# Causal attention in a four-batch transformer kernel: mask inside the row maximum, quotients formed in the transposed layout

## The chip, the cores and the metric

The kernel runs on one core of a Trainium2 chip. The metric is the device time of one execution in microseconds (us); lower is better. One core has TensorE (PE, matrix products, its results go to PSUM banks of 128 partitions by 512 f32 values), VectorE (DVE), ScalarE (ACT), GpSimd (POOL), SyncE (SP) that issues transfers, and DMA engines. Each engine runs its own queue of instructions in order and waits for others through semaphores.

## The reference

Four sequences of 1024 tokens with 256 channels go through two transformer layers in f32, each followed by a residual sum and layer norm.

```python
x = _layernorm(x + _L0_attn_ref(x, ...))   # 16 heads of 16, no mask, q and k normed, rope
x = _layernorm(x + _L0_ffn_ref(x, ...))    # SiLU gate, 256 -> 768 -> 256
x = _layernorm(x + _L1_attn_ref(x, ...))   # 8 heads of 32, causal
x = _layernorm(x + _L1_ffn_ref(x, ...))    # 16 experts, two per token, at most 512 tokens each
```

The change concerns the third line mostly:

```python
def _L1_attn_ref(x, w_qkv, w_out, head_scales):
    B, T, C = x.shape                      # 4, 1024, 256
    H = N_HEADS                            # 8
    hd = C // H                            # 32
    scale = 1.0 / math.sqrt(hd)
    qkv = (x @ w_qkv).reshape(B, T, 3, H, hd)
    q = jnp.transpose(qkv[:, :, 0], (0, 2, 1, 3))
    k = jnp.transpose(qkv[:, :, 1], (0, 2, 1, 3))
    v = jnp.transpose(qkv[:, :, 2], (0, 2, 1, 3))
    scores = jnp.einsum('bhqd,bhkd->bhqk', q, k) * scale
    causal = jnp.tril(jnp.ones((T, T), dtype=bool))
    scores = jnp.where(causal[None, None], scores, -jnp.inf)
    q_proj = jnp.einsum('bhtd,hd->bht', q[..., :3], dirs)
    k_proj = jnp.einsum('bhtd,hd->bht', k[..., :3], dirs)
    geo = q_proj[..., :, None] * k_proj[..., None, :]
    scores = scores + head_scales[None, :, None, None] * geo
    attn = jax.nn.softmax(scores, axis=-1)
    out = jnp.einsum('bhqk,bhkd->bqhd', attn, v).reshape(B, T, C)
    return out @ w_out
```

The geometric term is a product of one number per query and one per key, so the kernel folds it into the query projection's weights, and the products of q and k already hold it.

## The kernel before, in words

All instructions up to the experts are ordered by hand: the order in which the program is written is the order in each engine's queue. A stage is a generator of "units" (some PE work with what hangs on it), and `weave` (L1145) runs the units of one stage and puts the "pieces" of another between them: each call of a piece issues a few matrix products and their followers. `later(n, fn)` (L116) puts a small step of DVE or POOL on a list; `tick` (L119), once per unit, issues the steps that are due. PSUM has eight banks: a ring of six, tag "s", that nearly all products take in turn, and one each for values and denominators (`ps_av`, `ps_m`).

The four batches pass one after the other through first attention (`first_units`, L1051), second attention (`second_units`, L1103), the SiLU FFN and the routing; `weave` joins one batch's attention with the other pieces of its own batch or of a neighbour. Near the end, L1344 weaves batch 3's second attention, with projection and routing pieces of batch 2 in it and, from unit 30, the first pieces of batch 3's own projection and routing. L1348 issues what is left before the last tokens are sent to the experts.

A second attention works on two groups of four heads. It has 36 units:

- Twelve head units (a "head" below is this opening stretch of an attention, not an attention head): `Maxima1.unit` of group 0 alone.
- Twelve units of group 0: the scores (L969), values (L1004) and, beside them, the maxima of group 1.
- Twelve units of group 1: scores and values alone.

`Maxima1.unit` (L923) forms, for 128 queries and up to 512 keys of four heads, the products in four banks (L931). Units on the diagonal (8 of 12, with 128, 256, 384 or 512 keys) then add a triangle of large negative numbers to the last 128 columns, by one matrix product of `ident_h` and `mask_h` per head (L940). DVE takes the negated row maximum of each bank into `part` (L942). `split` and `turn` put the maxima into a layout in which PE subtracts them as part of the scores.

`scores` lays keys on partitions and 512 queries along the bank; ACT takes the exponential (L989) into `pe`, POOL clears what lies above the diagonal (L992). `values` (L1015) adds up two banks over the key blocks: the value products `av`, with heads and channels on partitions and tokens along the bank, and the denominators `dn` in the same layout, each repeated over the 32 channels of its head. After the last key block ACT copies both banks to SBUF (L1025). `unload` (L1028), one or two units later, turns them with eight PE transposes into a layout with tokens on partitions (L1033), DVE takes the reciprocal of the denominators (L1036) and multiplies (L1037) into `oq1`.

`out_project` (L540) serves both layers. A "turn" transposes four blocks of the quotients back to channels on partitions (L549) and ACT copies them (L552); a "project" multiplies by the output weights (L559), and `add_residual` (L515) adds on DVE and starts the layer norm.

At the start of the program `project_qk` squares q and k on POOL (L230) and sums the squares on DVE (L233); the square has one buffer, tag "sq", which the sine table also uses.

Of the kernel before, what the change touches and what calls it, by code (L numbers as in the profile page):

```python
# [35 lines left out]
def postln_layers_kernel(ctx: ExitStack, tc: tile.TileContext, a: dict, out: bass.AP):  # L36
# [8 lines left out]
    mask_h = const.tile([P, P], BF16, name="mask_h")  # L45
    nc.gpsimd.memset(mask_h, 0.0)
    nc.gpsimd.affine_select(
        out=mask_h, in_=mask_h, pattern=[[-1, P]], compare_op=ALU.is_ge, fill=NEG, base=0, channel_multiplier=1
    )
    neg_half = const.tile([P, 1], F32, name="neg_half")  # L50
# [51 lines left out]
    with ExitStack() as main:  # L102
# [45 lines left out]
        sinT = fa.tile([P, TB, D0], F32, tag="sq", bufs=1, name="sinT")  # L148
# [54 lines left out]
        def project_qk(b, pr, first=False):  # L203


            def piece(j, big):
# [21 lines left out]
                def squares():  # L228
                    sq = fa.tile([P, 512], F32, tag="sq", bufs=1, name=f"sq0_{b}_{pr}_{j}")
                    nc.gpsimd.tensor_tensor(sq, x, x, ALU.mult)  # L230

                    def sums():
                        nc.vector.tensor_reduce(part, sq.rearrange("p (h d) -> p h d", d=D0), AX.X, ALU.add)  # L233

                    return sums
# [135 lines left out]
        class Maxima:  # L371


            def __init__(self, b, g, engines):
# [7 lines left out]
                def rotate(s, u):  # L382
# [3 lines left out]
                    y = fa.tile(  # L386
                        [P, 4, 4, D0], F32, tag="tmp" if eng is nc.gpsimd else "sq", bufs=1, name=f"y0_{b}_{g}_{s}_{u}"
                    )
# [123 lines left out]

        mvs, open_rows = {}, set()
# [26 lines left out]
        def out_project(b, oqs, w, name):  # L540
# [3 lines left out]
            def turn(h, c, big):  # L544
                if c == 0:
                    oTs[h] = act.tile([P, 2, 512], F32, tag="hT", bufs=1, name=f"oT{name}_{b}_{h}")
                pt = bank(f"pt{name}_{b}_{h}_{c}", big)
                for i in range(4):
                    nc.tensor.transpose(  # L549
                        pt[:, i * P : (i + 1) * P], oqs[b][:, 4 * h + i, c * P : (c + 1) * P], ident  # L550
# [3 lines left out]
            def project(j, big):  # L554
                ps = bank(f"pp{name}_{b}_{j}", big)
                for i in range(2):
                    q = slice((2 * j + i) % 4 * P, ((2 * j + i) % 4 + 1) * P)
                    for c in range(2):
                        nc.tensor.matmul(  # L559
                            ps[:, i * 256 : (i + 1) * 256], oTs[j // 2][:, c, q], w[:, c, :], start=c == 0, stop=c == 1  # L560
                        )
                for i in range(2):
                    add_residual(b, 2 * j + i, ps[:, i * 256 : (i + 1) * 256], name)
# [5 lines left out]
            return out  # L569

# [302 lines left out]
        def wait(big):  # L873
            pass

# [39 lines left out]
        class Maxima1:  # L915
# [7 lines left out]
            def unit(self, i):  # L923
# [5 lines left out]
                for h in range(4):  # L929
# [6 lines left out]
                        stop=not diag,  # L936
                    )
                if diag:
                    for h in range(4):
                        nc.tensor.matmul(scs[h][:, n - P : n], ident_h, mask_h, start=False, stop=True)  # L940
                for h in range(4):
                    nc.vector.tensor_reduce(self.part[:, t, u, h : h + 1], scs[h][:, :n], AX.X, ALU.max, negate=True)  # L942
# [20 lines left out]
        class Attend1:  # L963


            def __init__(self, m, oq):
                self.m, self.oq, self.b, self.g, self.pes, self.avs = m, oq, m.b, m.g, {}, {}
# [36 lines left out]
            def values(self, i):  # L1004
# [17 lines left out]
                if kt == 4 * qb + 3:  # L1022
                    for k in range(2):
                        d = act.tile([P, 512], F32, tag="avs", bufs=2, name=f"avs1_{self.b}_{self.g}_{qb}_{k}")
                        nc.scalar.copy(d, self.av[k])  # L1025
                        self.avs[qb, k] = d

            def unload(self, qb):  # L1028
                pt = [ps_s.tile([P, 512], F32, tag="s", name=f"pto1_{self.b}_{self.g}_{qb}_{k}") for k in range(2)]
                for k in range(2):  # L1030
                    for t in range(4):
                        q = slice(t * P, (t + 1) * P)
# [515 lines left out]
```

## Time and profile before

| | us |
|---|---|
| runs | 2515.32, 2517.42, 2521.31 |
| median | 2517.42 |
| the profiled execution | 2514.16 |
| its span in the profile | 2512.3 |
| around the span (difference) | 1.9 |
| PE busy in the span | 2360.3 (94%) |
| DVE busy | 1366.7 (54%) |
| ACT busy | 1023.4 (41%) |
| POOL busy | 730.5 (29%) |

The profile is of one execution. Its mean granted clock of PE is 0.959 of full speed. A group line of the profile reads: code line, engine, operation, output<-input with partitions x elements, number of instructions, then busy time and mean ns of one, then the idle time of the engine just before them and who ended it. In the time line, the first number is the start and the second the duration of one instruction or of a run of equal ones (the last field gives how many), and the brackets hold the idle time before it. A wait line gives who waited for whom, total us, how often, and the longest.

### The profile page before, as it was taken

Reading aid. Unit: us, or ns where it says so; the run is one execution under the profiler, and the core shown is the slowest. Engines: PE = TensorE matmul, PEld = TensorE weight load, DVE = VectorE, ACT = ScalarE, POOL = GpSimd, SP = SyncE. Lnnn points to the kernel's source line nnn. Section 1 sums busy time; section 2 is a strip of 40 time slices with the busy share of each in tenths; the row PEclk is TensorE's granted clock in tenths of the full one; section 3 lists DMA queues with packets and bytes.
Section 4 is the critical chain, followed back from the end, with each engine's and each line's share of the span. In section 5 each row is a group of like instructions: output and inputs, shape, how many; then the busy total and the mean of one; then the engine's idle time right before and its main releaser. Section 6 shows DMA issues by size and latency. Waiting matters only on the chain.

```text
span 2512.3 us, 36681 instructions
## 1 busy us (share of the span) xinstructions
PE 2360.3 (94%) x14452; PEld 1193.2 (47%) x14452; DVE 1366.7 (54%) x3161; ACT 1023.4 (41%) x2011; POOL 730.5 (29%) x1015
## 2 busy tenths in 40 slices
PE   6999999999999999999999999999999983999994
PEld 3333334444445543444455434445556442666662
DVE  6765654766657447787563677817535565111113
ACT  1355554555552345545424455472331340111112
POOL 5623623425024112454131320211110143112223
PEclk8999999999998999999989999999998985999997
DMA  3134212000000000001100000102000012444434
GB/s 89 33 120 136 82 61 83 1 27 1 1 1 27 1 1 1 23 24 54 31 1 1 1 1 1 41 28 98 1 1 1 1 52 68 101 101 118 103 88 145
DMA packets 79628, 109.89 MB, mean 44 GB/s; under 512 B 8800, under 2 KB 68448, under 8 KB 77792
## 3 DMA queue, kind: packets, MB, share of 16 engines
q1 hardware_dynamic: 54080, 80.21, 9.8%
q0 software_dynamic: 9984, 14.82, 3.1%
q10 hardware_dynamic: 15392, 12.53, 1.7%
q8 instruction: 113, 1.85, 0.3%
q14 instruction: 59, 0.48, 0.1%
HBM read 68.64 MB, written 38.90 MB: 43 GB/s over the span
## 4 chain that ended last, share of the span: by engine, by line
PE 85%; DVE 8%; POOL 2%; DMA 2%; issue 1%; ACT 1%; SPq 0%; ACTq 0%; POOLq 0%; DVEq 0%
PE sc L458 19%; PE av L476 10%; PE ph L1410 7%; PE py L1426 7%; PE gu L595 7%; PE mx L434 4%; PE sc L978 4%; PE mx L931 4%; PE p L898 4%; PE dn L611 4%; PE av L1015 3%; PE dn L1015 2%; DVE part L942 2%; PE qk L298 2%; PE ppa L559 2%; PE pt L425 2%
## 5 line engine op out<-in xcount | busy, mean ns | idle before, releaser
L437 DVE TENSOR_REDUCE part<-mx 128x1 f32<-128x512 f32 x1024 | 656.3, 684 | 340.6 <-PE mx L434 334.8
L467 ACT ACTIVATE pe<-sc 128x512 f32<-128x512 f32 x1024 | 554.1, 596 | 392.9 <-PE mx L434 338.0
L434 PE MATMUL mx<-kT,qT 32*128 32x512 f32 x2048 | 650.3, 643 | 5.7 <-DVE part L437 5.5
L458 PE MATMUL sc<-qT,kT 32*128 32x512 f32 x2048 | 614.6, 636 | 0.2 <-ACT pe L467 0.2
L458 PEld LDWEIGHTS sc<-qT,kT 32*128 32x128 f32 x2048 | 181.7, 183 | 223.1 <-issue 177.0
L476 PE MATMUL av<-pe,va 128*32 128x512 f32 x2048 | 272.7, 605 | 0.0
L942 DVE TENSOR_REDUCE part<-mx 128x1 f32<-128x512 f32 (+3 forms) x384 | 186.8, 549 | 152.2 <-PE mx L940 108.6
L434 PEld LDWEIGHTS mx<-kT,qT 32*128 32x128 f32 x2048 | 196.5, 184 | 53.6 <-DVE part L437 28.2
L989 ACT ACTIVATE pe<-sc 128x512 f32<-128x512 f32 (+3 forms) x384 | 157.6, 499 | 156.6 <-PE sc L978 156.4
L1410 PE MATMUL ph<-dmT,f 128*128 128x512 f32 x384 | 170.2, 602 | 4.3 <-DVE dmT L90 3.5
L1426 PE MATMUL py<-f,hTm 128*128 128x256 f32 x768 | 167.7, 379 | 0.0
L1418 ACT ACTIVATE hTm<-ph,b 128x512 f32<-128x512 f32 x96 | 60.8, 684 | 261.3 <-PE ph L1410 261.3
L992 POOL TENSOR_SCALAR_AFFINE_SELECT pe<-pe 128x256 f32<-128x256 f32 x128 | 51.9, 412 | 373.9 <-ACT pe L989 371.7
L1426 PEld LDWEIGHTS py<-f,hTm 128*128 128x128 f32 x768 | 145.9, 190 | 25.0 <-issue 5.7
L1430 POOL DMA_INDIRECT acc_d<-yo,dm x48 | 74.5, 1553 | 284.8 <-DVE yo L1428 238.9
L931 PE MATMUL mx<-kT,qT 32*128 32x512 f32 (+3 forms) x768 | 138.6, 592 | 8.2 <-DVE part L942 4.8
L356 POOL TENSOR_TENSOR ss<-ss,neg_half 128x16 f32<-128x16 f32 x48 | 138.8, 2909 | 0.5
L1427 DVE TENSOR_TENSOR yo<-py,b 128x256 f32<-128x256 f32 x48 | 20.4, 425 | 210.3 <-PE py L1426 210.3
L476 PEld LDWEIGHTS av<-pe,va 128*32 128x32 f32 x2048 | 40.3, 108 | 192.6 <-issue 182.6
L978 PE MATMUL sc<-qT,kT 32*128 32x512 f32 (+3 forms) x768 | 118.3, 547 | 1.7 <-DVE part L942 0.6
L1410 PEld LDWEIGHTS ph<-dmT,f 128*128 128x128 f32 x384 | 72.8, 192 | 94.8 <-issue 86.7
L595 PE MATMUL gu<-xTf,wg 128*128 128x256 f32 x384 | 106.8, 400 | 0.0
(357 smaller groups left out, 2935.2 us busy)
## 6 DMA issues: line engine op xcount, KB each, us to landing
f<-in_fc SPq DMA_DIRECT2D x14, 1024.0 KB, 5.0
f<-in_fc ACTq DMA_DIRECT2D x10, 1024.0 KB, 5.7
xink<-in_xT SPq DMA_DIRECT2D x32, 256.0 KB, 3.7
disp_d<-empty SPq DMA_DIRECT2D x12, 520.0 KB, 6.1
qk_d<-xs SPq DMA_DIRECT2D x6, 1024.0 KB, 4.3
xr<-qk_d SPq DMA_DIRECT2D x6, 1024.0 KB
dm<-disp_d SPq DMA_DIRECT2D x11, 520.0 KB, 3.6
xinv<-in_xT SPq DMA_DIRECT2D x16, 256.0 KB, 4.8
```

The costliest lines, as they stand in the source:

```text
L434: nc.tensor.matmul(sc, self.qT[r, t * P : (t + 1) * P], self.kT[r, u * 512 : (u + 1) * 512], start=True, stop=True)
L437: return lambda: nc.vector.tensor_reduce(self.part[:, t, u, h : h + 1], sc, AX.X, ALU.max, negate=True)
L458: nc.tensor.matmul(sc, self.m.kT[r, kt * P : (kt + 1) * P], self.m.qT[r, qb * 512 : (qb + 1) * 512], start=True, stop=True)
L467: nc.scalar.activation(self.pes[i, h // 2][:, h % 2, :], sc, AF.Exp)
L476: nc.tensor.matmul(self.av[32 * h : 32 * h + 32, :], va0[:, kt, 4 * self.g + h, :], self.pes[i, h // 2][:, h % 2, :], start=kt == 0, stop= ...
L595: nc.tensor.matmul(ps[:, i * 256 : (i + 1) * 256], w[:, c, f * P : (f + 1) * P], xT[j][:, c, :], start=c == 0, stop=c == 1,)
L931: nc.tensor.matmul(scs[h][:, :n], qT[r, t * P : (t + 1) * P], kT[r, u * 512 : u * 512 + n], start=True, stop=not diag,)
L942: nc.vector.tensor_reduce(self.part[:, t, u, h : h + 1], scs[h][:, :n], AX.X, ALU.max, negate=True)
L978: nc.tensor.matmul(scs[h][:, off:], ones_h[r, :] if w else kT[r, kt * P : (kt + 1) * P], (self.m.nmT if w else qT)[r, q], start=w == 0, st ...
L989: nc.scalar.activation(pe[:, j, off:], scs[2 * hp + j][:, off:], AF.Exp)
L1410: nc.tensor.matmul(ph[:, i * CAP : (i + 1) * CAP], f1[:, c, (f + i) * P : (f + i + 1) * P], dmT[:, c, :], start=c == 0, stop=c == 1,)
L1426: nc.tensor.matmul(py[:, :C], hT[:, f, c * P : (c + 1) * P], f2[:, f, :], start=f == 0, stop=f == FF1 // P - 1)
```

## The change

- The mask joins the row maximum. A constant `mask_w` of 128x512 holds zeros and, in its last 128 columns, the triangle. On diagonal units DVE adds it to the bank and takes the maximum in one call, `tensor_tensor_reduce` (add, scale by -1, minimum), whose elementwise result goes to a scratch tile `masked` that nobody reads. In the instruction stream a call is two DVE instructions, the main one and one that reads the accumulator out. The 256 mask products on PE are gone.
- The quotients are formed where the value products lie. `unload` is gone. ACT copies denominators, then values, to SBUF, and in the following units four `divide` steps, a quarter (128 tokens) each, take a reciprocal of 128x128 on DVE and multiply on POOL, into `oT1`, with channels on partitions.
- The second layer's projection reads `oT1` directly. Its turns and their ACT copies are gone; two empty pieces take their place in the order. `out_project` becomes `out_project0` (first layer, unchanged in what it issues) and `out_project1`.
- The squares, the sine table and one rope product move from a tag with one buffer to a tag with two.

```diff
     make_identity(nc, ident)
-    mask_h = const.tile([P, P], BF16, name="mask_h")
-    nc.gpsimd.memset(mask_h, 0.0)
+
+    mask_w = const.tile([P, 512], BF16, name="mask_w")
+    nc.gpsimd.memset(mask_w, 0.0)
     nc.gpsimd.affine_select(
-        out=mask_h, in_=mask_h, pattern=[[-1, P]], compare_op=ALU.is_ge, fill=NEG, base=0, channel_multiplier=1
+        out=mask_w[:, 384:512],
+        in_=mask_w[:, 384:512],
+        pattern=[[-1, P]],
+        compare_op=ALU.is_ge,
+        fill=NEG,
+        base=0,
+        channel_multiplier=1,
     )
+    masked = const.tile([P, 512], BF16, name="masked")
     neg_half = const.tile([P, 1], F32, name="neg_half")
...
         nc.scalar.dma_start(cosT, a["cos"].rearrange("(t p) d -> p t d", p=P))
-        sinT = fa.tile([P, TB, D0], F32, tag="sq", bufs=1, name="sinT")
+        sinT = act.tile([P, TB, D0], F32, tag="q1", bufs=G1, name="sinT")
         nc.scalar.dma_start(sinT, a["sin"].rearrange("(t p) d -> p t d", p=P))
...
                 def squares():
-                    sq = fa.tile([P, 512], F32, tag="sq", bufs=1, name=f"sq0_{b}_{pr}_{j}")
+                    sq = act.tile([P, 512], F32, tag="q1", bufs=G1, name=f"sq0_{b}_{pr}_{j}")
                     nc.gpsimd.tensor_tensor(sq, x, x, ALU.mult)
...
                     x = xr[:, ts, s, hs, :]
-                    y = fa.tile(
-                        [P, 4, 4, D0], F32, tag="tmp" if eng is nc.gpsimd else "sq", bufs=1, name=f"y0_{b}_{g}_{s}_{u}"
-                    )
+                    if eng is nc.gpsimd:
+                        y = fa.tile([P, 4, 4, D0], F32, tag="tmp", bufs=1, name=f"y0_{b}_{g}_{s}_{u}")
+                    else:
+                        y = act.tile([P, 4, 4, D0], F32, tag="q1", bufs=G1, name=f"y0_{b}_{g}_{s}_{u}")
                     z = fa.tile([P, 4, 4, D0], F32, tag="tmpz", bufs=1, name=f"z0_{b}_{g}_{s}_{u}")
...
+        def wait(big):
+            pass
+
...
-        def out_project(b, oqs, w, name):
+        def project_out(b, j, oT, w, name, big):
+
+            ps = bank(f"pp{name}_{b}_{j}", big)
+            for i in range(2):
+                for c in range(2):
+                    nc.tensor.matmul(
+                        ps[:, i * 256 : (i + 1) * 256], oT(c, i), w[:, c, :], start=c == 0, stop=c == 1
+                    )
+            for i in range(2):
+                add_residual(b, 2 * j + i, ps[:, i * 256 : (i + 1) * 256], name)
+
...
+        def out_project1(b):
+
+
+            def project(j, big):
+                project_out(b, j, lambda c, i: oT1[b][:, c, (2 * j + i) * P : (2 * j + i + 1) * P], w1o, "a1", big)
+
+            out = [lambda big, j=j: project(j, big) for j in range(4)]
+            return out[:2] + [wait, wait] + out[2:]
...
                         start=True,
-                        stop=not diag,
+                        stop=True,
                     )
-                if diag:
-                    for h in range(4):
-                        nc.tensor.matmul(scs[h][:, n - P : n], ident_h, mask_h, start=False, stop=True)
                 for h in range(4):
-                    nc.vector.tensor_reduce(self.part[:, t, u, h : h + 1], scs[h][:, :n], AX.X, ALU.max, negate=True)
+                    part = self.part[:, t, u, h : h + 1]
+                    if diag:
+                        nc.vector.tensor_tensor_reduce(
+                            masked[:, :n], scs[h][:, :n], mask_w[:, 512 - n :], -1.0, -NEG, ALU.add, ALU.min, part
+                        )
+                    else:
+                        nc.vector.tensor_reduce(part, scs[h][:, :n], AX.X, ALU.max, negate=True)
...
-            def __init__(self, m, oq):
-                self.m, self.oq, self.b, self.g, self.pes, self.avs = m, oq, m.b, m.g, {}, {}
+            def __init__(self, m, oT):
+                self.m, self.oT, self.b, self.g, self.pes = m, oT, m.b, m.g, {}
...
                 if kt == 4 * qb + 3:
-                    for k in range(2):
-                        d = act.tile([P, 512], F32, tag="avs", bufs=2, name=f"avs1_{self.b}_{self.g}_{qb}_{k}")
-                        nc.scalar.copy(d, self.av[k])
-                        self.avs[qb, k] = d
-
-            def unload(self, qb):
-                pt = [ps_s.tile([P, 512], F32, tag="s", name=f"pto1_{self.b}_{self.g}_{qb}_{k}") for k in range(2)]
-                for k in range(2):
-                    for t in range(4):
-                        q = slice(t * P, (t + 1) * P)
-                        nc.tensor.transpose(pt[k][:, q], self.avs[qb, k][:, q], ident)
-                p4 = [t.rearrange("p (t h d) -> p t h d", t=4, h=4) for t in pt]
-                rc = act.tile([P, 4, 4], F32, tag="rc", bufs=2, name=f"rc1_{self.b}_{self.g}_{qb}")
-                nc.vector.reciprocal(rc, p4[1][:, :, :, 0])
-                nc.vector.tensor_tensor(
-                    self.oq[:, 4 * qb : 4 * qb + 4, P * self.g : P * self.g + P].rearrange(
-                        "p t (h d) -> p t h d", h=4
-                    ),
-                    p4[0],
-                    rc.unsqueeze(3).to_broadcast([P, 4, 4, D1]),
-                    ALU.mult,
-                )
+
+                    vs, rc = [
+                        act.tile([P, 512], F32, tag="avs", bufs=2, name=f"{n}_{self.b}_{self.g}_{qb}")
+                        for n in ("avs1", "rc1")
+                    ]
+                    nc.scalar.copy(rc, self.av[1])
+                    nc.scalar.copy(vs, self.av[0])
+
+                    def divide(k):
+                        q = slice(k * P, (k + 1) * P)
+                        nc.vector.reciprocal(rc[:, q], rc[:, q])
+                        to = self.oT[:, self.g, qb * 512 + k * P : qb * 512 + (k + 1) * P]
+                        nc.gpsimd.tensor_tensor(to, vs[:, q], rc[:, q], ALU.mult)
+
+                    for k in range(4):
+                        later(min(1 + k, 3), lambda k=k: divide(k))
         groups = {}
-        oq0, oq1, ends = {}, {}, {}
+        oq0, oT1, ends = {}, {}, {}
         both_pool = (nc.gpsimd, nc.gpsimd)
...
-            oq1[b] = act.tile([P, TB, C], F32, tag="oq", bufs=2, name=f"oq1_{b}")
+            oT1[b] = act.tile([P, G1, S], F32, tag="oq", bufs=2, name=f"oT1_{b}")
             now = Maxima1(b, 0)
...
                 nxt = Maxima1(b, g + 1) if g + 1 < G1 else None
-                at = Attend1(now, oq1[b])
+                at = Attend1(now, oT1[b])
                 for i in range(12):
...
                         now.turn(1)
-                        if last is not None:
-                            last.unload(1)
                     if nxt is not None:
...
                             nxt.split(1)
-                    if i == 6:
-                        at.unload(0)
                     yield
             last.values(11)
-            last.unload(1)
...
         def first_end(b):
-            return [lambda big: ends[b](big)] + out_project(b, oq0, w0p, "a0")
+            return [lambda big: ends[b](big)] + out_project0(b)
         def second_end(b):
-            return out_project(b, oq1, w1o, "a1") + route(b)
+            return out_project1(b) + route(b)
...
         out2 = second_end(2)
-        straight(out2[:8] + project1(3))
-        out3 = out_project(3, oq1, w1o, "a1")
+        straight(out2[:6] + project1(3))
+        out3 = out_project1(3)
         st, tu, lo = route(3, True)
         steps2, sums2 = dispatch(2, True)
-        weave(second_units(3), 23, out2[8:], True, out3[:4] + st[:2], 30, steps2, 18)
+        weave(second_units(3), 23, out2[6:], True, out3[:2] + [wait] + st[:2], 31, steps2, 18)
         flush()
-        for piece in tu[:2] + out3[4:6] + lo[:2] + out3[6:]:
+        for piece in tu[:2] + lo[:2] + out3[4:]:
             piece(True)
```

More of the change, by code (lines that the diff above doesn't have):

```diff
@@ L538, in add_residual, with out_project0 @@
                 later(1, root)
-        def out_project(b, oqs, w, name):
+        def project_out(b, j, oT, w, name, big):
[7 more added lines that the diff above has]
+                add_residual(b, 2 * j + i, ps[:, i * 256 : (i + 1) * 256], name)
+        def out_project0(b):
             oTs = {}
@@ L545, in turn @@
                 if c == 0:
-                    oTs[h] = act.tile([P, 2, 512], F32, tag="hT", bufs=1, name=f"oT{name}_{b}_{h}")
-                pt = bank(f"pt{name}_{b}_{h}_{c}", big)
+                    oTs[h] = act.tile([P, 2, 512], F32, tag="hT", bufs=1, name=f"oTa0_{b}_{h}")
+                pt = bank(f"pta0_{b}_{h}_{c}", big)
                 for i in range(4):
                     nc.tensor.transpose(
-                        pt[:, i * P : (i + 1) * P], oqs[b][:, 4 * h + i, c * P : (c + 1) * P], ident
+                        pt[:, i * P : (i + 1) * P], oq0[b][:, 4 * h + i, c * P : (c + 1) * P], ident
                     )
@@ L554, in project, with oT @@
             def project(j, big):
[L555 to L560, printed above, removed]
-                        )
-                for i in range(2):
-                    add_residual(b, 2 * j + i, ps[:, i * 256 : (i + 1) * 256], name)
+                def oT(c, i):
+                    t = (2 * j + i) % 4
+                    return oTs[j // 2][:, c, t * P : (t + 1) * P]
+                project_out(b, j, oT, w0p, "a0", big)
             out = []
@@ L871, in postln_layers_kernel @@
         sent, based = [], []
-        def wait(big):
-            pass
         qTs, kTs, va1 = {}, {}, {}
@@ L1022, in values @@
                 if kt == 4 * qb + 3:
-                    for k in range(2):
-                        d = act.tile([P, 512], F32, tag="avs", bufs=2, name=f"avs1_{self.b}_{self.g}_{qb}_{k}")
-                        nc.scalar.copy(d, self.av[k])
-                        self.avs[qb, k] = d
-            def unload(self, qb):
-                pt = [ps_s.tile([P, 512], F32, tag="s", name=f"pto1_{self.b}_{self.g}_{qb}_{k}") for k in range(2)]
-                for k in range(2):
-                    for t in range(4):
-                        q = slice(t * P, (t + 1) * P)
-                        nc.tensor.transpose(pt[k][:, q], self.avs[qb, k][:, q], ident)
-                p4 = [t.rearrange("p (t h d) -> p t h d", t=4, h=4) for t in pt]
-                rc = act.tile([P, 4, 4], F32, tag="rc", bufs=2, name=f"rc1_{self.b}_{self.g}_{qb}")
-                nc.vector.reciprocal(rc, p4[1][:, :, :, 0])
-                nc.vector.tensor_tensor(
-                    self.oq[:, 4 * qb : 4 * qb + 4, P * self.g : P * self.g + P].rearrange(
-                        "p t (h d) -> p t h d", h=4
-                    ),
-                    p4[0],
-                    rc.unsqueeze(3).to_broadcast([P, 4, 4, D1]),
-                    ALU.mult,
-                )
+                    vs, rc = [
[11 more added lines that the diff above has]
+                        later(min(1 + k, 3), lambda k=k: divide(k))
         groups = {}
-        oq0, oq1, ends = {}, {}, {}
+        oq0, oT1, ends = {}, {}, {}
         both_pool = (nc.gpsimd, nc.gpsimd)
```

## The prediction

> **What bounds the kernel now.** I read the page first (shares of busy time, the chain that ended last, the costliest groups), then busy time by stretch around the second attention, then the waits of VectorE and TensorE there, then single instructions.
>
> ```profile
> span 2512.3 us, 36681 instructions
> PE 2360.3 (94%) x14452; PEld 1193.2 (47%) x14452; DVE 1366.7 (54%) x3161; ACT 1023.4 (41%) x2011; POOL 730.5 (29%) x1015
> PE 85%; DVE 8%; POOL 2%; DMA 2%; issue 1%; ACT 1%; SPq 0%; ACTq 0%; POOLq 0%; DVEq 0%
> ```
>
> TensorE (PE) is busy 94% of the span and holds 85% of the chain, so work taken off its queue normally shortens the run by that work. VectorE (DVE) holds the next 8%; the change loads that engine, so the stages where it is near its limit decide. Busy time by stretch: the "heads" of batches 0 to 3 (the twelve units of maxima that open a second attention), then of batch 0 its first and second head group:
>
> ```profile
> 756.80:789.00 32.20, 30.87 (x169) 17.89 (x165) 25.72 (x63) 4.03 (x7) 15.62 (x8) 0.84 0.16 51
> 1238.60:1272.80 34.20, 32.87 (x168) 18.98 (x164) 25.73 (x63) 4.03 (x7) 15.64 (x8) 0.75 0.18 56
> 1696.80:1735.20 38.40, 35.88 (x217) 22.86 (x214) 34.64 (x91) 4.67 (x9) 3.74 (x8) 0.96 0.45 159
> 1914.50:1948.90 34.40, 32.51 (x161) 19.86 (x160) 29.27 (x78) 1.76 (x3) 2.80 (x6) 0.75 0.00 0
> 789.00:862.00 73.00, 72.17 (x588) 35.18 (x592) 42.36 (x107) 28.83 (x68) 18.86 (x28) 0.98 0.01 1
> 862.00:915.00 53.00, 52.44 (x436) 29.24 (x428) 12.18 (x31) 21.83 (x54) 7.38 (x18) 1.00 0.00 1
> ```
>
> The columns are the window, its length, and the busy time of PE, weight loads, DVE, ACT and POOL, then PE's granted clock. In the heads DVE is busy 75 to 90% and the clock is 0.75 to 0.96: PE and DVE hand six banks to and fro. In the group stretches PE is full (72 of 73 us, 52 of 53) and DVE has room (42, then 12). One instruction more on DVE is near its full price in a head and near nothing behind it.
>
> **The change part by part.** (a) Masks. 256 mask matmuls, four per diagonal unit, leave PE. What a unit's four cost is read from the starts in the time line:
>
> ```profile
> 833.62 0.40 PE L940 MATMUL mx<-mask_h,ident_h 128*128 128x128 bf16 x4
> 833.86 0.65 PE L595 MATMUL gu<-xTf,wg 128*128 128x256 f32 x2
> 827.07 1.09 PE L1033 MATMUL pto<-ident,avs 128*128 128x128 f32 x8
> 828.00 1.03 PE L595 MATMUL gu<-xTf,wg 128*128 128x256 f32 x4
> 921.31 0.66 PE L549 MATMUL pta<-ident,oq 128*128 128x128 f32 x4
> 921.90 0.69 PE L458 MATMUL sc<-qT,kT 32*128 32x512 f32 x1
> ```
>
> Start to next start: 0.24 us a mask group, 0.93 us a turn of the quotients (L1033), 0.59 us a turn ahead of the projection (L549). Of 64 diagonal units 32 lie in group stretches where PE is full: 32 x 0.24 = 7.7 us gained.
>
> In the same units the row maximum becomes tensor_tensor_reduce, built as two DVE instructions: the add with the mask, and a read of the accumulator; the former also waits for the previous write of its scratch tile. The plain reduce:
>
> ```profile
> L942 DVE TENSOR_REDUCE part<-mx 128x1 f32<-128x512 f32 x192 | 119.1, 682 | 53.8 <-PE mx L931 43.3 <-PE mx L940 10.4
> L942 DVE TENSOR_REDUCE part<-mx 128x1 f32<-128x256 f32 x64 | 22.6, 417 | 13.8 <-PE mx L940 13.7
> ```
>
> The trace has no tensor_tensor_reduce. Call D the extra time of one masked maximum. Four 512-wide reduces take 2.48 us (start 763.62), 0.60 apart, so consecutive ones overlap by 0.08. A two-input operation on a bank and SBUF costs what a one-input one does (L520, 256 wide, 407 ns; the 256-wide reduce 417 ns). Lower end: only the read is added, as the copy of 128x4 between two row operations at 2025.38, for 0.07 us of queue; with 0.04 to 0.05 for lost overlap D = 0.12. Upper end: no overlap, both steps whole with a gap of 0.04 each: 0.68 + 0.04 + 0.17 + 0.04 - 0.60 = 0.33; I use 0.31, since the narrow forms have less to lose. I take D = 0.17, by the copy's row, which is nearest to a read of one value.
>
> Here a rule speaks against the change. The Trainium skill, page "VectorE: DVE Perf Modes", section "The DRAIN you can't avoid", says that a DVE operation does not start until the pipe of the one before has emptied, and its "Rules for kernel authors" ask for few operations rather than few waits. By that D is its upper end, 0.31. The trace's overlap of 0.08 and slot of 0.07 for a 0.16 us copy say that small followers cost less, so the row decides for the centre and the rule supplies the first rival. With 0.31 the sum below would be a loss.
>
> Heads: 4 x 32 x 0.17 = 21.8 us more DVE. Back come DVE's waits for masks:
>
> ```profile
> DVE part L942 <- PE mx L940: 4.3, 6, 2.2
> DVE part L942 <- PE mx L940: 5.1, 6, 2.2
> DVE part L942 <- PE mx L940: 19.9, 3, 18.4
> DVE part L942 <- PE mx L940: 23.2, 3, 22.3
> ```
>
> One line per head, batches 0 to 3; the longest is the wait before the head's first unit and stays, so 2.1 + 2.9 + 1.5 + 0.9 = 7.4 us. The mask groups also stand on PE ahead of later units; at the heads' clock one is 0.3 us, 32 are 9.6, and I count half, 4.8, because DVE also waits for the plain products there (3.2 us in the first head). Net loss 21.8 - 7.4 - 4.8 = 9.6 us.
>
> (b) Quotients. The 16 turns of eight go. Fifteen stand in full PE stretches: 15 x 0.93 = 14.0 us, and PE's wait for the copies ahead of them (pto on avs, 2.2 us by the waits) mostly goes: 1.7. The sixteenth is in the tail, under (e). In their place ScalarE copies the same two banks, in the other order: the value bank comes free some 0.6 us later. Its next user comes after the next unit's scores on PE, over 4 us, so nothing; without that cover 16 x 0.6 = 10 us. Per turn 0.255 + 0.692 = 0.95 us of DVE goes (L1036, L1037), and four reciprocals of 128x128 come. The exact shape has a row, 953 ns (L249), so 64 x 0.953 - 16 x 0.95 = 61.0 - 15.2 = +45.8 us of DVE. Each of 64 new POOL multiplies is as L393, 464 ns: 30 us on an engine at 29%. Affine selects queue behind them and values behind those; POOL has 50 us free of 73, so I give it nothing (16 x 0.5 = 8 us if one per turn were exposed). The quarters are due within three ticks and the two buffers are wanted again four or five units later, so ScalarE's next copies don't wait.
>
> (c) Exposed DVE work outside the heads: 45.8 + 128 x 0.17 = 67.6 us, beside full PE. PE's own waits on DVE are small there (none among those of batch 0's two groups), and DVE keeps 30 us free per group stretch. But a reciprocal of 1 us sits ahead of maxima whose banks PE wants. Ends: nothing, and half (34 us). I take a tenth, 6.8, nearer the lower end as the six banks give about one unit of slack.
>
> (d) Projection. Of 16 second-layer turns (L549) 14 leave full stretches: 14 x 0.59 = 8.3 us; their ScalarE copies (588 ns each) lay beside. Projections now depend on POOL's products, one stage behind their quarter; the two empty pieces keep the distance. Nothing, or 0.5 us each at 16 projections, 8 us, if POOL were late.
>
> (e) Ends. At the start, squares lie in one buffer:
>
> ```profile
> 12.99 1.04 POOL L230 TENSOR_TENSOR sq<-xr 128x512 f32<-128x512 f32 x1 [8.49 <-DVE rope_x L177]
> 18.51 1.04 POOL L230 TENSOR_TENSOR sq<-xr 128x512 f32<-128x512 f32 x1 [4.48 <-DVE ss L233]
> 20.42 1.04 POOL L230 TENSOR_TENSOR sq<-xr 128x512 f32<-128x512 f32 x1 [0.86 <-DVE ss L233]
> 22.32 1.04 POOL L230 TENSOR_TENSOR sq<-xr 128x512 f32<-128x512 f32 x1 [0.86 <-DVE ss L233]
> ```
>
> With two, POOL need not wait 0.86 us per square, and the sine table no longer shares: the last sum should end about 21.2 instead of 24.1, 2.9 us on a serial chain. The DMA that loads the table keeps its place in ScalarE's queue; the wider mask costs POOL a longer fill while it waits 8.49 us anyway. At the end of batch 3 one turn of quotients and two ahead of the projection go from the chain that leads to routing: 0.93 + 2 x 0.59 = 2.1; I count 2.0, as POOL's sends stand before its last products.
>
> **Sum.** Gains 7.7 + 14.0 + 1.7 + 8.3 + 2.9 + 2.0 = 36.6; losses 9.6 + 6.8 = 16.4; net 20.2. The profiled execution took 2514.16, of which 1.9 lie around the span of 2512.3; it becomes 2494.0 with a span of 2492.1. It stands 3.3 under the median of 2517.42, from which the same step gives 2497.
>
> **Rivals.** *VectorE becomes the bound.* Place: the heads. Price: at D = 0.31 they lose 39.7 - 12.2 = 27.5; outside, 39.7 us of masked maxima, half exposed as PE starves for banks, 19.9; reciprocals 6.8 as nothing better is known; less 36.6, so +17.6, 2535. It decides from about D = 0.25 (19.8 + 12.8 + 6.8 = 39.4 against 36.6, at four tenths exposed). For it: DVE at 90% in the third head, the added wait on the scratch tile, the rule above. Against: 0.07 us for a small copy. Chance 0.22, spread 2518 to 2540.
>
> *Freed PE time turns into waits.* PE stops less for masks and turns, but sooner for banks, exponentials and selects; half the gain stays: 36.6/2 = 18.3, less the heads' 9.6, so -8.7: 2509. For it: affine selects already hold values up (4.4 us by the waits). Against: ACT is at 40% and POOL at 26% of the group stretch. Chance 0.12.
>
> *The change doesn't remove what it says:* excluded for PE, since the changed code issues no mask product and no second-layer turn; only the start's 2.9 and the tail's 2.0 could fail (2502).
>
> **How the numbers follow.** Forecast 0.66, own range 2484 to 2511: below, D = 0.12 and nothing exposed, 6 + 7 us; above, D = 0.22 or 14 us exposed. About 0.2% (5 us) is what a measurement of this kernel can tell from no change. Of the forecast 0.63 is faster and 0.03 within; of the second rival 0.09 faster, 0.02 within, 0.01 slower; of the first 0.02 within, 0.20 slower. The range 2482 to 2526 leaves out 0.05 below and some 0.13 of the first rival above.
>
> **What would show it.** Accumulator reads near 0.17 us or less and four masked 512 maxima in 3.0 to 3.3 us: right; above 3.6, first rival. Heads 2 to 3 us longer each. Batch 0's first group stretch about 4 us shorter with PE still 97% busy; a fall to 93% with waits of mx on part or of av on pe would be the second rival. Reciprocals at 0.95 us; last start-up sum at 21 us. Wrong altogether if the masked maximum runs at half rate (1.2 us for 512): at a mean width of 320 and (682 - 417)/256 = 1.04 ns an element 128 x 0.33 = 43 us more in the heads alone.

## The result, and the profile after

The changed kernel takes 2537.22 us (median of 4 runs, 2536.97 to 2539.80) against 2517.56 us before (4 runs): 1.0084 times as long, 95% interval 1.0072 to 1.0096. The prediction was 2497 us and faster; the time lies outside its range.

The head of the page after, and the chain by engine:

```profile
span 2535.3 us, 36343 instructions
PE 2367.6 (93%) x14004; PEld 1181.4 (47%) x14004; DVE 1430.7 (56%) x3449; ACT 1015.3 (40%) x1995; POOL 761.8 (30%) x1079
PE 83%; DVE 10%; POOL 2%; DMA 2%; issue 1%; ACT 1%; ACTq 0%; SPq 0%; DVEq 0%; POOLq 0%
```

Two of these numbers seem to contradict each other: PE has 448 matmul records fewer and is busy 7 us longer. So a matmul's busy time in this profile is not work alone. The 384 products of 512 columns for the maxima (L931 before, L956 after) are the same in both kernels and show 726 ns each before, 797 after.

The medians differ by 19.7 us, the spans of the two profiled executions by 23.0. The table says where the 23 us went, worked out from the starts of the stages in both traces. A head here ends at the first exponential of its attention, and the second group begins with its own first exponential. "Between" is from the end of the last product of values and denominators of one second attention to the first product for the maxima of the next; for the most part this is the next batch's first attention.

| stage | before | after, difference |
|---|---|---|
| start and first attention of batch 0 | 756.8 | -4.2 |
| the four heads | 153.3 | +12.2 |
| first groups, four | 270.2 | +3.5 |
| second groups, batches 0 to 2 | 170.8 | -4.1 |
| second group, batch 3 | 43.1 | +3.2 |
| the three stretches between | 662.5 | +12.3 |
| from there to the end | 455.5 | +0.1 |

The heads of batches 0 to 3 by the windows' busy time (PE, weight loads, DVE, ACT, POOL, then PE's granted clock), and below them batch 3's head before. PE shows as busy for 92 to 97% of each, its clock is down to 0.55 in batch 3's head (0.73 before), and DVE has some 8 us free at most:

```profile
752.70:792.10 39.40, 38.13 (x152) 22.85 (x148) 31.86 (x105) 4.62 (x8) 16.80 (x10) 0.68 0.13 42
1242.80:1282.30 39.50, 38.21 (x152) 22.68 (x148) 31.36 (x102) 4.65 (x9) 16.81 (x10) 0.70 0.15 49
1707.60:1754.70 47.10, 43.11 (x214) 26.38 (x210) 41.19 (x134) 5.32 (x11) 3.74 (x8) 0.96 0.37 130
1929.80:1969.20 39.40, 38.16 (x141) 22.24 (x140) 33.05 (x113) 1.76 (x3) 2.80 (x6) 0.55 0.00 1
```

```profile
1914.50:1952.10 37.60, 35.71 (x177) 21.59 (x176) 31.85 (x86) 2.35 (x4) 2.80 (x6) 0.73 0.00 1
```

The new instructions' groups, and below them DVE's time line in the first head, after and then before:

```profile
L966 DVE CUSTOM_DVE_ANT_0 masked<-mx,mask_w 128x512 bf16<-128x512 f32 x64 | 44.2, 691 | 16.3 <-PE mx L956 8.8
L966 DVE DVE_READ_ACCUMULATOR2_ANT part<- 128x1 f32 x256 | 21.3, 83 | 0.1
L1061 DVE RECIPROCAL rc<-rc 128x128 f32<-128x128 f32 x64 | 58.1, 929 | 12.8 <-ACT rc L1056 7.8 <-POOL pe L1020 5.1
L1063 POOL TENSOR_TENSOR oT<-avs,rc 128x128 f32<-128x128 f32 x64 | 29.5, 462 | 154.1 <-DVE rc L1061 148.0 <-DVE lg L719 4.5 <-DVE lg L808 1.1
```

```profile
760.52 0.69 DVE L966 CUSTOM_DVE_ANT_0 masked<-mx,mask_w 128x512 bf16<-128x512 f32 x1
761.14 0.08 DVE L966 DVE_READ_ACCUMULATOR2_ANT part<- 128x1 f32 x1
761.36 0.69 DVE L966 CUSTOM_DVE_ANT_0 masked<-mx,mask_w 128x512 bf16<-128x512 f32 x1
761.98 0.08 DVE L966 DVE_READ_ACCUMULATOR2_ANT part<- 128x1 f32 x1
```

```profile
763.62 2.48 DVE L942 TENSOR_REDUCE part<-mx 128x1 f32<-128x512 f32 x4 [0.45 <-PE mx L940]
```

By durations alone, 691 and 83 ns, a masked maximum looks cheap. The starts tell its price: 760.52 to 761.36 is 0.84 us, against 0.60 for a plain one. The read ends at 761.22, and 0.14 us pass before the next main instruction. So D was some 0.245, at the point (0.25) from which the first rival was to decide. The median spacings in the traces give the same D at every width: 443, 577, 710 and 844 ns for 128, 256, 384 and 512 columns, against 198, 331, 465 and 598 before.

The start of the program did what was foreseen. The last two of the four squares stand together, and POOL is done at 20.5 us where it was 23.4:

```profile
18.49 2.04 POOL L238 TENSOR_TENSOR sq<-xr 128x512 f32<-128x512 f32 x2 [3.06 <-DVE ss L241]
```

### The profile page after: what moved, and what is told of

It reads as the page before. It is cut to its first block, busy times and chain, and to the rows that moved or that the text cites. A ratio compares the mean times of both kernels' runs of the same rounds, so it can differ in the third digit from the quotient of the medians.

```text
span 2535.3 us, 36343 instructions
## 1 busy us (share of the span) xinstructions
PE 2367.6 (93%) x14004; PEld 1181.4 (47%) x14004; DVE 1430.7 (56%) x3449; ACT 1015.3 (40%) x1995; POOL 761.8 (30%) x1079
## 4 chain that ended last, share of the span: by engine, by line
PE 83%; DVE 10%; POOL 2%; DMA 2%; issue 1%; ACT 1%; ACTq 0%; SPq 0%; DVEq 0%; POOLq 0%
PE sc L467 19%; PE av L485 9%; PE ph L1427 7%; PE gu L623 7%; PE py L1443 7%; PE mx L443 5%; PE sc L1006 4%; PE mx L956 4%; PE p L923 4%; PE dn L639 4%; PE av L1043 3%; PE dn L1043 2%; PE qk L306 2%; PE ppa L557 2%; PE pt L434 2%
## 5 line engine op out<-in xcount | busy, mean ns | idle before, releaser
L443 PE MATMUL mx<-kT,qT 32*128 32x512 f32 x2048 | 659.1, 640 | 5.5 <-DVE part L446 5.0
L443 PEld LDWEIGHTS mx<-kT,qT 32*128 32x128 f32 x2048 | 199.4, 184 | 60.5 <-DVE part L446 32.0
L966 DVE CUSTOM_DVE_ANT_0 masked<-mx,mask_w 128x128 bf16<-128x128 f32 (+3 forms) x256 | 125.6, 491 | 113.3 <-PE mx L956 84.3
L956 PE MATMUL mx<-kT,qT 32*128 32x512 f32 (+3 forms) x768 | 158.9, 643 | 7.8 <-DVE part L970 2.6
L1006 PE MATMUL sc<-qT,kT 32*128 32x512 f32 (+3 forms) x768 | 129.8, 562 | 4.5 <-DVE x L532 3.0
L956 PEld LDWEIGHTS mx<-kT,qT 32*128 32x128 f32 x768 | 75.5, 217 | 71.4 <-issue 20.7
```

The costliest lines, as they stand in the source:

```text
L443: nc.tensor.matmul(sc, self.qT[r, t * P : (t + 1) * P], self.kT[r, u * 512 : (u + 1) * 512], start=True, stop=True)
L956: nc.tensor.matmul(scs[h][:, :n], qT[r, t * P : (t + 1) * P], kT[r, u * 512 : u * 512 + n], start=True, stop=True,)
L1006: nc.tensor.matmul(scs[h][:, off:], ones_h[r, :] if w else kT[r, kt * P : (kt + 1) * P], (self.m.nmT if w else qT)[r, q], start=w == 0, st ...
```

## The experiments

The first four take the change apart.

**Mask part alone**, with the tag (edit: the diff's mask, maxima and tag hunks).

> The kernel before with the mask inside the row maximum, and the two-buffer tag of the squares (its room is needed for the wider mask), but with the old quotients, turns and projection. Theory A (VectorE in the heads): each masked maximum costs 0.245 us more, the four heads grow by about 12 us as they did after the change, and the mask products on PE gave next to nothing back; with about 4 us from the tag: 2525 to 2529 us. Theory B (the loss lies in the quotients and in where the projection's pieces fall): the mask part is no loss, 2508 to 2515 us.

Measured 2529.60 us, 0.6 us above theory A's range, ratio 1.0055 (1.0041 to 1.0069). Heads +14.9, first groups +5.1, between +0.8. Theory A holds for this part in time and place: against the tag alone (2512.16 us, below), the mask inside the maximum costs 17.4 us. Its clause that the products on PE gave next to nothing back doesn't hold: with the tag and no mask at all the time is 2501.18 us (at the end of this section), so the products were worth 11.0 us, and the masked maxima cost 28.4.

**Quotients alone** (edit: the diff's other hunks).

> The changed quotients, divide steps and projection without turns alone; mask products on PE and the one-buffer tag as before. Theory A (all loss is VectorE's masked maxima): PE has 24 us less to do, 2495 to 2505 us. Theory B (the first attention of the next batch doesn't gain from fewer turns, and its pieces fall in worse places): the stretches between the second attentions grow by 5, 5 and 2 us and batch 3's second group by 4, against 4 us less in the second groups of batches 0 to 2: 2524 to 2530 us.

Measured 2528.33 us, ratio 1.0045 (1.0031 to 1.0059). Heads -1.3, second groups of batches 0 to 2 -4.1, of batch 3 +3.0, between +14.5. Theory B holds for this part. So each theory was right for one part, and the largest terms of the two parts lie in different stages. Alone they lose 13.4 and 12.1 us, 25.5 together, where the whole change loses 19.7; why it is nearly 6 us less, no run shows.

**Tag alone** (edit: the diff's three tag hunks).

> Only the squares, the sine table and the rope product get the tag with two buffers. Both theories: the first sum of squares ends 2.8 us earlier, and with the clock's early low stretch shorter the first attention starts 4.1 us earlier: 2513 to 2515 us. If the 4 us are something else's (the mask's longer fill, chance), 2516 to 2518 us.

Measured 2512.16 us, ratio 0.9983 (0.9974 to 0.9991): 4.0 us gained, the only part of the change that pays as it stands.

**No mask in the maxima**, on the kernel before.

> The kernel before with no mask in the maxima at all: neither products on PE nor an addition on VectorE (a row's maximum then is over all keys of its unit, which only shifts the exponents; the clearing after the exponential stays). It prices the 256 mask products. The prediction's reckoning: 7.7 us in the group stretches, 7.4 and 4.8 in the heads, 2497 to 2500 us. Theory C (a unit lasts as long as the six banks go round, and PE fills the rest with waiting that shows as busy): only VectorE's waits in the heads come back, 2508 to 2512 us.

```diff
-                        stop=not diag,
+                        stop=True,
                     )
-                if diag:
-                    for h in range(4):
-                        nc.tensor.matmul(scs[h][:, n - P : n], ident_h, mask_h, start=False, stop=True)
```

Measured 2505.81 us, ratio 0.9956 (0.9943 to 0.9970), 10.4 us faster: between the two ranges, nearer theory C's. First groups -4.1, heads -4.8. That is about half of the 19.9 us that the prediction's reckoning gave.

The next two repair one thing each in the changed kernel.

**Result written into the bank.**

> The changed kernel, but the masked maximum writes its elementwise result back into the bank it reads (the scratch tile is gone), so that no masked maximum waits for the one before. Theory A1 (the 0.15 us between an accumulator's read and the next masked maximum is the wait for the scratch tile): the spacing of four 512-wide ones falls from 0.845 to 0.70 to 0.75 us, the heads get 8 to 12 us shorter, 2525 to 2530 us. Theory A2 (the gap belongs to the accumulator's read itself): spacing stays at 0.82 to 0.86 us, 2535 to 2539 us.

```diff
-    masked = const.tile([P, 512], BF16, name="masked")
...
                         nc.vector.tensor_tensor_reduce(
-                            masked[:, :n], scs[h][:, :n], mask_w[:, 512 - n :], -1.0, -NEG, ALU.add, ALU.min, part
+                            scs[h][:, :n], scs[h][:, :n], mask_w[:, 512 - n :], -1.0, -NEG, ALU.add, ALU.min, part
```

Measured 2515.33 us, ratio to the kernel before 0.9995 (0.9986 to 1.0004), 21.9 us below the changed kernel, lower than theory A1's range. Its time line in the first head:

```profile
762.54 0.73 DVE L965 CUSTOM_DVE_ANT_0 mx<-mx,mask_w 128x512 f32<-128x512 f32 x1
763.19 0.14 DVE L965 DVE_READ_ACCUMULATOR2_ANT part<- 128x1 f32 x1
763.19 0.73 DVE L965 CUSTOM_DVE_ANT_0 mx<-mx,mask_w 128x512 f32<-128x512 f32 x1
763.84 0.14 DVE L965 DVE_READ_ACCUMULATOR2_ANT part<- 128x1 f32 x1
```

Both instructions became longer, 0.73 and 0.14 us, and yet the spacing fell from 0.84 to 0.65 us: the read now overlaps the next main instruction (both start at 763.19). Heads -3.0 against before, where they were +12.2; between stays at +11.9.

**Empty pieces in place of the turns.**

> The changed kernel with empty pieces where the second layer's projection turns were, so that every other piece falls in the unit where it fell before the change. Theory B1 (pieces that fall into worse units): the stretches between second attentions lose the 12.3 us they had gained, 2523 to 2527 us. Theory B2 (the divide steps on VectorE and POOL delay the first attention): they stay, 2534 to 2538 us.

```diff
-            return out[:2] + [wait, wait] + out[2:]
+            return [wait, wait] + out[:2] + [wait, wait] + out[2:]
...
-        straight(out2[:6] + project1(3))
+        straight(out2[:8] + project1(3))
...
-        weave(second_units(3), 23, out2[6:], True, out3[:2] + [wait] + st[:2], 31, steps2, 18)
+        weave(second_units(3), 23, out2[8:], True, out3[:4] + st[:2], 30, steps2, 18)
...
-        for piece in tu[:2] + lo[:2] + out3[4:]:
+        for piece in tu[:2] + lo[:2] + out3[6:]:
```

Measured 2522.32 us, just under theory B1's range, ratio 1.0027 (1.0012 to 1.0041), 14.9 us below the changed kernel. The six executions fall into two groups, 2516.80 to 2519.36 and 2525.28 to 2527.95, so the 14.9 is uncertain by some 5 us; the trace is of the first group (2517.80). In it the stretches between went from +12.3 to -3.3. Theory B1: with as many divide steps on the same engines, the loss is gone once the other pieces are back in their units.

What a "worse unit" is can be read unit by unit in batch 1's first attention. The table is worked out from PE's time line; a unit runs from one start of value products (av) to the next. The names are PE's products of a unit beside the attention's own: pta and ppa are turn and projection of the second layer, ptn, pl and pos belong to the routing, ptxf and dn to the FFN, pt_1a and pto to the first attention itself.

```
unit  before                        after                      empty pieces
  0   4.0  pta x4                   5.2  ppa x8                4.0
  1   4.0  pta x4                   6.5  ppa x8                4.0
 16   4.0  ptn x4                   4.8  pl x8                 4.0  ptn x4
 17   4.0                           4.0                        4.0
 18   4.7  pt_1a x4 + pl x8         4.8  pt_1a x4              4.8  pt_1a x4 + pl x8
 34   6.2  pt_1a + pos + ptxf       8.2  pt_1a + pos + dn x12  6.2  pt_1a + pos + ptxf
 35   5.9  dn x12                   4.0                        5.9  dn x12
 36   6.5  pto x4 + dn x12          9.4  pto x4 + dn x12       6.5  pto x4 + dn x12
```

A unit with a turn and one with nothing last 4.0 us; of this batch's four turns only one stands in a longer unit, of 4.5 us. The turn fits into time that the unit takes anyway, so leaving it out gains next to nothing. In the kernel before, two starts of av around a turn and two around nothing look alike in the time line:

```profile
919.24 1.06 PE L476 MATMUL av<-pe,va 128*32 128x512 f32 x8
921.31 0.66 PE L549 MATMUL pta<-ident,oq 128*128 128x128 f32 x4
923.23 1.07 PE L476 MATMUL av<-pe,va 128*32 128x512 f32 x8
...
998.07 1.06 PE L476 MATMUL av<-pe,va 128*32 128x512 f32 x8
1002.06 1.07 PE L476 MATMUL av<-pe,va 128*32 128x512 f32 x8
```

And the slack is per unit; what one doesn't use, another can't. Before, pt_1a and pl shared a unit of 4.7 us; after, each has its own at 4.8, and the pair takes one slack more. In unit 36 DVE was still in the chain of routing steps that unit 34's pos had released when the FFN's products wanted a bank that DVE had to read first, and PE waited 2.83 us (line of the time line after):

```profile
1098.87 2.83 PE L639 MATMUL dn<-wd,hT 128*128 128x256 f32 x12 [2.83 <-DVE oq L504]
```

The trace also shows why DVE was so late there. Four small steps of the chain took 0.60 to 0.71 us where the others take 0.17, 1.9 us more in sum. They didn't start late; each ended 0.02 to 0.03 us after one of four POOL products of 128x256 that ran beside it. The first two, with POOL's:

```profile
1093.37 0.60 DVE L810 TENSOR_SCALAR keep<-pk 128x8 f32<-128x8 f32 x1
1094.09 0.71 DVE L812 TENSOR_SCALAR step<-ei 128x8 f32<-128x8 f32 x1
1093.21 0.73 POOL L404 TENSOR_TENSOR y<-xr,rope_gc 128x256 f32<-128x256 f32 x1
1094.03 0.74 POOL L406 TENSOR_TENSOR y<-y,z 128x256 f32<-128x256 f32 x1
```

In the kernel before, the same chain ran beside a POOL instruction of 128x16 and its steps took 0.17 us each. So a moved piece can also bring two engines' steps together that were apart before.

A third cost lies in batch 3's second group. PE waited there for a bank of the projection that DVE had yet to read, in the waits after:

```profile
PE sc L1006 <- DVE x L532: 3.0, 3, 2.5
```

The longest of the three, 2.5 us, ends at 2065.8 us. DVE ran steps of batch 2's dispatch until 2064.4 us and read the projection's banks only then; before, it had stood idle for 4.8 us when the projection came. With the empty pieces each projection comes a unit later, this wait is gone, and batch 3's second group is +0.2 us in place of +3.2.

POOL's late products, to which an expectation below puts this loss down, show elsewhere: batch 2's projection, just ahead of batch 3's second attention, waited for them three times, 4.1 us in all (the line `PE ppa L557 <- POOL oT L1063: 4.1, 3, 1.6` of the waits). That stretch is 2.0 us longer than before. With the empty pieces these waits are gone, but PE waits there once, for 4.5 us, until DVE has added a projection to `x`, and the stretch is still 1.2 us longer.

**Is it the wait on the write before?** Writing into the bank also changed the memory that is written, so two scratch tiles in turn separate the two.

> The changed kernel with two scratch tiles of one byte an element, used in turn, in place of one of two bytes: each masked maximum still carries a wait on its own engine, but for the one before last. Theory W (the 0.2 us is the stall on the write just before): the spacing of four 512-wide ones is 0.65 us as with the write into the bank, 2513 to 2519 us. Theory S (any wait on its own engine, or any write to SBUF beside the accumulator, costs it): 0.84 us, 2534 to 2539 us.

```diff
-    masked = const.tile([P, 512], BF16, name="masked")
+    masked2 = [const.tile([P, 512], mybir.dt.uint8, name=f"masked{i}") for i in range(2)]
...
-                            masked[:, :n], scs[h][:, :n], mask_w[:, 512 - n :], -1.0, -NEG, ALU.add, ALU.min, part
+                            masked2[h % 2][:, :n], scs[h][:, :n], mask_w[:, 512 - n :], -1.0, -NEG, ALU.add, ALU.min, part
```

Measured 2511.26 us, 1.7 us below theory W's range, ratio 0.9980 (0.9972 to 0.9988), 26.0 below the changed kernel. Heads -6.8 against before; between, which this repair leaves alone, +17.0. The time line of the first head:

```profile
761.08 0.69 DVE L966 CUSTOM_DVE_ANT_0 masked<-mx,mask_w 128x512 uint8<-128x512 f32 x1
761.69 0.08 DVE L966 DVE_READ_ACCUMULATOR2_ANT part<- 128x1 f32 x1
761.69 0.69 DVE L966 CUSTOM_DVE_ANT_0 masked<-mx,mask_w 128x512 uint8<-128x512 f32 x1
```

The spacing is 0.61 us, a plain reduce's 0.60 within a hundredth, though it still writes to SBUF. Theory W: a wait on the masked maximum two back costs nothing that shows, on the one just before 0.23 us. (The elements are one byte wide here in place of two; this run alone doesn't exclude that the width plays a part, but the write into the bank has four bytes and shows nearly the same.)

**Both repairs together**, by way of the bank, and then by two scratch tiles.

> The changed kernel with both repairs: the masked maximum writes back into its bank, and empty pieces stand where the projection's turns were. If the two losses are independent, their repairs (21.9 and 14.9 us below the changed kernel's 2537.2) add up: 2499 to 2503 us. If they overlap in the heads or in batch 3: 2505 to 2515 us.

> The changed kernel with two scratch tiles in turn and with the empty pieces in place of the turns. If both repairs stay independent: the two scratch tiles' 2511.3 less the 15 to 19 us that the empty pieces brought to the two other versions, 2492 to 2497 us, level with the version without any mask (2491.9). If the late steps of the first attentions (17 us in the run with two scratch tiles) are not all a matter of where pieces fall: 2498 to 2505 us.

Measured 2496.17 us, ratio 0.9921 (0.9908 to 0.9935), and 2496.64 us, ratio 0.9921 (0.9908 to 0.9935). The first is below the range of full additivity by 3 us; the second lies at the upper end of its first range. By two scratch tiles the repairs add up (26.0 + 14.9 = 40.9 us, measured 40.6); by way of the bank they bring 4 us more than their sum (36.8, measured 41.1), within what the spread of the empty pieces' run leaves open. Together they take away more than twice the changed kernel's loss of 19.7 us.

**Versions without any mask in the maxima.**

> The kernel before with the two-buffer tag and with no mask in the maxima (a row's maximum is over all keys of its unit); old quotients, turns and projection. If the two gains add up, 4.0 and 10.4 us below the kernel before: 2501 to 2503 us. If the gains meet at the same stretch (the heads' clock), 2504 to 2508 us.

> The changed kernel with no mask in the maxima and with the empty pieces in place of the turns. Theory B1: the new quotients are then worth what the second groups show, 1.1 us each for three batches, and some 3 us more in the first groups, against batch 3's late products (3 us): 2498 to 2503 us. Theory B2: 2510 to 2514 us.

Measured 2501.18 us, ratio 0.9941 (0.9927 to 0.9955), and 2491.92 us, ratio 0.9908 (0.9893 to 0.9923). The first lies in the range of two gains that add up. The second is better than its range under B1 and is the fastest kernel of this study, 24.2 us under the kernel before beside which it ran (2516.16) and 45.3 under the changed one. The new quotients with the empty pieces are worth 9.3 us (2501.18 - 2491.92). The masked maxima with two scratch tiles cost 4.7 us over no mask (2496.64 - 2491.92), less than the 11.0 us of the products on PE that they replace. So both halves of the change seem to pay once they are repaired; no run has the new quotients, the empty pieces and the old products together, so the 6 us between these two is an estimate from different kernels.

## Why the prediction was wrong

The sum's parts against the runs, in us (a gain is positive):

| part of the sum | forecast | measured |
|---|---|---|
| mask: 7.7 - 9.6 | -1.9 | -17.4 |
| quotients and projection: 14.0 + 1.7 + 8.3 + 2.0 - 6.8 | +19.2 | -12.1, with the empty pieces +9.3 |
| start | +2.9 | +4.0 |

Three steps failed: the price of a masked maximum, the reading of PE time from start to start, and the place of the pieces, which the sum doesn't have.

**The price of a masked maximum (a).** D was taken as 0.17 with ends 0.12 and 0.31; it was 0.245. The wait on the scratch tile stood in the text, but the 0.17 has no term for it; only the upper end has gaps, of 0.04 us each. Without the wait D is 0.01 to 0.05, below my lower end. By the prediction's own formula the heads lose 31 - 12.2 = 19 us at 0.24; they lost 12.2, and the mask part as a whole 17.4. The signs that the prediction named couldn't tell the cases apart: four masked maxima of 512 took 3.23 us and the heads grew by 1.8 to 4.3 us each, both near what was to show it right, while the first groups behind the heads, where the masks were to gain 7.7, lost 5.1 with the mask part alone. The rule that I weighed there, that the pipe empties between operations, was not what decided: without the wait the next main instruction starts before the one in front has ended (761.69 against 761.77 with two scratch tiles), as the Trainium skill's page "VectorE: DVE Perf Modes" itself allows in that section, "The DRAIN you can't avoid", for an operation that isn't held. The page goes on, in the same section, that a semaphore between chained operations costs nothing extra, measured on eight copies. For copies that may hold; here the trace with the wait on the instruction just before shows 0.84 us and those without it 0.61 and 0.65, so for this instruction the measurement decides against it.

**PE time read from start to next start (a, b, d).** The 7.7 us for masks in group stretches came out as 4.1 (no mask, first groups), the 12.2 us in the heads as 4.8. The 8.3 us for turns ahead of the projection came out near nothing where it could be read, in batch 1's first attention: 4.0 us a unit with and without for three turns, 0.5 us gained at the fourth. The turns of the quotients did pay: 4.1 us in three second groups, where two each stood, against 5.6 by my reckoning. What failed is the first reading, "PE is full (72 of 73 us)". The Trainium skill, page "Perfetto Trace Analysis", section "Identifying the Most-Contended Engine", says that busy time of matmuls is no good measure of how near a kernel is to PE's peak, because they are pipelined. This trace agrees, with 448 matmul records fewer and 7.3 us more of busy time; so none of the PE terms could stand on the windows' busy shares alone.

**Where the pieces fall (d).** The prediction said that the two empty pieces "keep the distance". They did for the projection's halves; but six pieces in place of eight move every later piece of the stage to another unit. This term is missing from the sum. It was +12.3 us in the stretches between, and three pairs of runs with and without the empty pieces put it at 14.9, 19.2 and 14.6 us of the whole. POOL's late products were put at nothing, with 8 us as the other end; PE's waits for them came to 4.1 us, all in one stretch that grew by 2.0.

**What held.** The start: 2.9 us forecast, last sum 2.8 us earlier, 4.0 us in the timed runs. The reciprocals at 0.93 us each and POOL's products at 0.46, as taken from the neighbouring rows. The reciprocals' exposure (6.8) can't be told apart, but is small: with the empty pieces and no mask every stage is below before or within 0.2 us of it, but for the short stretch ahead of batch 3's second attention (+2.5).

**The rivals.** The first was the right one for the mask's part of the loss, with place and threshold; it named the wait on the scratch tile among its reasons, but took its price from the rule of the emptying pipe. That its 2535 us lies close to the measured time is luck, since half of the loss came from the order of the pieces. The second, that half of the freed PE time stays as gain, was near the truth for the gains: 11.0 us of the 19.9 for the mask products and, with the empty pieces, 9.3 of the 26.0 for quotients and projection, the cost of the reciprocals taken off. What I lacked was a rival on the order of the pieces.

That both repairs end at 2496 us, beside the forecast of 2497, is no merit of the sum: its gains were too high and its D without the wait too.

## What to carry to other kernels

A result that nobody reads still has to be written, and the next instruction with the same scratch tile waits for it, on the same engine too: give it two tiles, or write over the operand. Before counting an instruction's removal as gain, compare two neighbouring units with and without it, from the same mark to the same mark; only what the unit's length shows is there to be had. When pieces are taken out of a hand-woven order, leave empty ones in their places first, and move the rest only as an edit of its own.

## What the runs showed of the hardware

A masked maximum on DVE that waits for the one just before it loses 0.23 us (0.84 us from start to start, against 0.61 when it waits for the one two back). The mask and the accumulator's read together cost 0.01 to 0.05 us over a plain maximum when nothing holds them, since the next main instruction starts together with the read. Writing the elementwise result over the operand in PSUM costs 0.04 us more than to SBUF (0.65 against 0.61).

PE's granted clock fell though PE showed 97% busy: time at half clock over the run was 205 us before and 260 after, in the four heads 51 and 88, and 0.55 is the mean clock of batch 3's head after. Whether the lower clock lengthened the heads by itself, or only shows that PE stood waiting for DVE, no run separates; that stays open. Half clock and length don't simply go together: with two scratch tiles the heads have 64 us of it, more than before, and are 6.8 us shorter.

Small DVE steps of the routing on 128x8 values take 0.17 us, but can last longer beside a POOL instruction. The trace after has 13 of 0.30 us or more, the one before five; each of the 18 ended 0.02 to 0.03 us after a POOL instruction on 128x128 or 128x256. By what means POOL holds them, no run shows.
